# Sixteen rounds of a recommendation kernel: a hardware loop written out, with ids loaded ahead

## The chip, the cores and the metric

The kernel runs on one core of one Trainium2 chip. The metric is the device time of one execution in microseconds: 16,796.05 us is the median of three runs before the change (16,795.29 to 16,816.24). A separate execution was recorded by the hardware profiler; the trace and all rows below are from it.

## The reference, cut to what matters

There are 16,384 samples with 69 user ids and one label id each, and a table `emb` of 100,001 rows of 96 floats.

```python
u = emb[batch_user]                       # [B, 69, 96]
ql = emb[batch_label[:, 0]]               # [B, 96]
q = broadcast(ql[:, None, :])
z = concatenate([q, u, q - u, q * u], -1) # [B, 69, 384]
h = dice(z @ W1 + b1, a1)                 # 64 wide; dice(x) = (a*(1-p) + p)*x, p = sigmoid(x)
att = (h @ W2 + b2) @ W3 + b3             # one weight per (sample, field)
pre = where(batch_user < 100000, u * att, 0)
pooled = einsum('gf,bfe->bge', window, pre)   # 69 fields into 10 groups
x = concatenate([pooled, ql], -1)         # [B, 1056]
y = dice(bn(x @ Wf1 + bf1)) -> dice(bn(. @ Wf2 + bf2)) -> . @ Wf3 + bf3
```

## The kernel before, in words

Tokens are the (sample, field) pairs in order. A block is 128 samples, which is 8,832 tokens or 69 tiles of 128 tokens. Eight blocks make a round, and sixteen rounds make the batch; the rounds are a hardware loop (`tc.For_i`, L406), so the program holds the instructions of one round, and every engine branches back at its end.

At the head of a round SyncE loads `ids` (L408), the 552 columns of user ids and 8 columns of label ids that the round needs, into a pool with one buffer, and VectorE makes `mask` from it (L410), which is 1 where an id counts. `res` (one row of 1,024 outputs) is stored by SyncE at the round's end (L429).

Every embedding row is brought by GpSimd, with one indirect DMA for 128 rows, all of them from one line (`gather`, L226): one for the block's labels (`q`) in `block_head`, and one for each tile of tokens (`u`) in `pair_part1`, 70 in a block and 560 in a round. The tiles are handled in nine pairs of chunks (a chunk is up to four tiles). `upool` has ten buffers of one pair each, so gathers may run some nine pairs ahead of their use.

`block_head` transposes `q` (L238), and makes the label's part of the first layer for each chunk (L246, L247). `pair_part1` transposes the gathered tiles on TensorE (L293), copies them to SBUF on ScalarE (L294), multiplies them by the label's row on VectorE (L262, L271), forms the hidden layer in `ph` (L298, L299) and applies Dice (L308 to L310). `pair_part2` forms the attention weights `patt` (L321, L323), scales the pooling windows `rw` (L331, L339) and adds the pooled sums into `acc` (L358), which VectorE copies out (L366). `top_net` (L377 to L403) is run once for each block, as a chain of small steps on TensorE, VectorE and ScalarE.

The pairs are software-pipelined: part 2 of a pair is written after part 1 of the next (`pend`, `finish`). Inside a round this goes on over block ends. At the end of a round `finish(pend)` is called with nothing beside it, then the result is stored, and the loop's branch follows. The order on each engine is made by a scheduler from the code; dependences between engines are semaphores. A gather also waits on one of eight semaphores that the gather eight places before it has used.

Of the kernel before, what the change touches and what calls it, by code (L numbers as in the profile page):

```python
"""DIN-style recommendation model (target attention over 69 fields, windowed pooling, Dice MLP).

Tokens are the (sample, field) pairs in row-major order. A block is 128 samples = 8832 tokens
= 69 tiles of 128 tokens; every offset inside a block depends on shapes alone.

Per tile of 128 tokens, one indirect DMA brings the embedding rows (tokens on partitions), and
TensorE transposes them. With Wq, Wu, Wd, Wp the four row blocks of W1,
    z @ W1 + b1 = u @ (Wu - Wd) + (q * u) @ Wp + (q @ (Wq + Wd) + b1),
where the last term is one row per sample. It rides in the first product: the rows of the samples
of a chunk (at most 9) lie below Wu - Wd in the stationary operand, and constant sample indicators  # L10
lie below u in the moving one.
    att = dice @ (W2 @ W3) + (b2 @ W3 + b3)
comes out with tokens on partitions, as the pooling needs it: for a tile,
    pooled[e, (sample, g)] += sum_token u[token, e] * att[token] * window[g, field(token)],
with window spread over the (at most 3) samples that the tile touches.
"""
# [18 lines left out]
P = 128  # L35
# [16 lines left out]
#: Chunks of tiles, two to a pair: the halves of the 128 partitions that H1 = 64 leaves.  # L52
# [3 lines left out]
#: Groups of samples whose pooled sums share a PSUM bank.  # L56
# [11 lines left out]
def sample_rows():  # L68
    """[NS, tokens]: 1 where a token belongs to the chunk's n-th sample."""
    rows = np.zeros((NS, BLK * F), np.float32)  # L70
    for ch, s0 in zip(CHUNKS, S0):
        at = np.arange(ch[0] * P, (ch[-1] + 1) * P)
        rows[at // F - s0, at] = 1.0
    return rows


def tile_samples():
    """[P, NT, 3]: 1 where a tile's p-th token belongs to the tile's n-th sample."""
    at = np.arange(BLK * F)
    n = at // F - (at // P * P) // F  # L80
    return np.eye(3, dtype=np.float32)[n].reshape(NT, P, 3).transpose(1, 0, 2).copy()
# [3 lines left out]
def rec_kernel(  # L85
# [31 lines left out]
    # The attention net's weights.  # L117
# [36 lines left out]
    # W2 @ W3, once for each half of the partitions, and b2 @ W3 + b3.  # L154
# [14 lines left out]
    # The pooling windows of the samples of each tile.  # L169
    R = const.tile([P, NT, 3 * G], F32, name="R")  # L170

    # The top net's weights.
# [43 lines left out]
    ipool = ctx.enter_context(tc.tile_pool(name="ipool", bufs=1))  # L216
# [16 lines left out]
    def block_head(bi, ids):  # L233
        """The block's labels: qT, and the rows q @ (Wq + Wd) + b1 of each chunk's samples."""
        q = bpool.tile([P, E], F32, tag="q", name=f"q{bi}")
        gather(q, ids[:, NB * NT + bi : NB * NT + bi + 1])
        pq = ps_m.tile([E, BLK], F32, tag="m", name=f"pq{bi}")
        nc.tensor.transpose(pq, q, ident)  # L238
        qT = bpool.tile([E, BLK], F32, tag="qT", name=f"qT{bi}")
        nc.vector.tensor_copy(qT, pq)  # L240
        per = 6
        for k0 in range(0, NCH, per):
            pc = ps_m.tile([P, per, H1], F32, tag="m", name=f"pc{bi}_{k0}")
            for k in range(per):
                s0 = S0[k0 + k]
                nc.tensor.matmul(pc[E : E + NS, k, :], qT[:, s0 : s0 + NS], Cq, start=True, stop=True)  # L246
            nc.vector.tensor_tensor(  # L247
                caug[bi % 2][E : E + NS, k0 : k0 + per, :],
                pc[E : E + NS],
                b1r[E : E + NS].to_broadcast([NS, per, H1]),  # L250
                ALU.add,
            )
        return qT

    def times_q(dst, src, t0, n, qT):
        """dst = src * q over a chunk's tokens, t0 the first token in the block."""
# [22 lines left out]
    def pair_part1(bi, pr, ids, qT):  # L279
        """Gather, transpose, and the attention net's hidden layer: its Dice outputs."""  # L280
# [32 lines left out]
    def pair_part2(bi, pr, mask, u, y, acc):  # L313
        """Attention weights, and the pooled sums of the pair's tiles."""
# [91 lines left out]
    with tc.For_i(0, NIT, 1) as it:  # L406
        ids = ipool.tile([P, NB * (NT + 1)], I32, name="ids")
        nc.sync.dma_start(out=ids, in_=idx[bass.ds(it, 1)].rearrange("o p n -> (o p) n"))  # L408
        mask = ipool.tile([P, NB * NT], F32, name="mask")
        nc.vector.tensor_scalar(mask, ids[:, 0 : NB * NT], float(ITEM_NUM), None, ALU.is_lt)  # L410
        res = ipool.tile([1, NB * BLK], F32, name="res")

        def finish(pend):
            bi, pr, u, y, acc, qT = pend
            pair_part2(bi, pr, mask, u, y, acc)
            if pr == NCH // 2 - 1:
                top_net(bi, acc["pooled"], qT, res)

        pend = None
        for bi in range(NB):  # L420
            qT = block_head(bi, ids)
            acc = {"pooled": bpool.tile([E, G, BLK], F32, tag="pooled", name=f"pooled{bi}")}
            for pr in range(NCH // 2):
# [3 lines left out]
                pend = (bi, pr, u, y, acc, qT)  # L427
        finish(pend)
        nc.sync.dma_start(out=out_v[bass.ds(it, 1)], in_=res)  # L429
# [42 lines left out]
```

## Time and profile before

| | |
|---|---|
| runs, median of 3 | 16,796.05 us |
| lowest, highest | 16,795.29, 16,816.24 us |
| profiled execution, first to last instruction (span) | 12,197.5 us |
| the profiled execution's own time beside its span | not given by the page |
| median less the span | 4,598.55 us |
| TensorE, matmuls busy | 11,517.2 us, 94% |
| GpSimd busy | 8,693.8 us, 71% |
| VectorE busy, ScalarE busy | 3,956.7 us and 3,145.7 us |
| mean granted TensorE clock | 0.693 of full speed |

The span counts from the first to the last instruction that the profiler saw. The medians are of executions that were not profiled. Busy time of an engine is the time in which one of its instructions runs; time between two instructions is told by the view of waits, with what seems to have ended it.

### The profile page before, as it was taken

Reading aid. Unit: us, or ns where it says so; the run is one execution under the profiler, and the core shown is the slowest. Engines: PE = TensorE matmul, PEld = TensorE weight load, DVE = VectorE, ACT = ScalarE, POOL = GpSimd, SP = SyncE. Lnnn points to the kernel's source line nnn. Section 1 sums busy time; section 2 is a strip of 40 time slices with the busy share of each in tenths; the row PEclk is TensorE's granted clock in tenths of the full one; section 3 lists DMA queues with packets and bytes.
Section 4 is the critical chain, followed back from the end, with each engine's and each line's share of the span. In section 5 each row is a group of like instructions: output and inputs, shape, how many; then the busy total and the mean of one; then the engine's idle time right before and its main releaser. Section 6 shows DMA issues by size and latency. Waiting matters only on the chain. (4 is left out here: it accounts for less than half of the span.)

```text
span 12197.5 us, 145905 instructions
## 1 busy us (share of the span) xinstructions
PE 11517.2 (94%) x56708; PEld 7206.8 (59%) x56708; DVE 3956.7 (32%) x12194; ACT 3145.7 (26%) x5536; POOL 8693.8 (71%) x8966
## 2 busy tenths in 40 slices
PE   8999999999999999999999999999999999999999
PEld 5655656566565665656656566565565655656556
DVE  2333323333232333333323333333333333333333
ACT  2222222222222222222222222222222222222222
POOL 6767677676776767767677676776767767677676
PEclk7677767666676776666766676676766767666677
DMA  1111111111111111111111111111111111111111
GB/s 43 40 35 39 36 38 39 35 39 35 38 39 34 39 35 39 39 33 39 35 39 39 34 39 35 39 40 35 39 35 39 40 35 39 33 40 39 34 39 34
DMA packets 293219, 456.88 MB, mean 37 GB/s; under 512 B 145632, under 2 KB 146834, under 8 KB 292530
## 3 DMA queue, kind: packets, MB, share of 16 engines
q0 software_dynamic: 286720, 440.98, 17.3%
q8 instruction: 464, 7.60, 0.3%
q1 hardware_dynamic: 4144, 5.09, 0.2%
q14 instruction: 225, 1.84, 0.1%
q10 hardware_dynamic: 1666, 1.37, 0.0%
HBM read 446.79 MB, written 0.07 MB: 37 GB/s over the span
## 5 line engine op out<-in xcount | busy, mean ns | idle before, releaser
L226 POOL DMA_INDIRECT u<-in_emb,ids x8832 | 8569.7, 970 | 2691.6 <-issue 2459.1
L298 PE MATMUL ph<-uT,caug 105*64 105x512 f32 (+2 forms) x4608 | 3101.9, 808 | 2.6 <-ACT uT L294 2.0
L299 PE MATMUL ph<-quT,w 96*64 96x512 f32 (+2 forms) x4608 | 3019.7, 796 | 0.4 <-DVE quT L271 0.4
L358 PEld LDWEIGHTS acc<-rw,u 128*96 128x96 f32 x18176 | 2515.6, 237 | 608.1 <-issue 234.7
L293 PEld LDWEIGHTS ptr<-ident,u 128*96 128x96 f32 x8832 | 1225.2, 164 | 2467.1 <-issue 1781.1
L358 PE MATMUL acc<-rw,u 128*96 128x30 f32 (+2 forms) x18176 | 2565.7, 305 | 33.2 <-DVE rw L339 32.3
L293 PE MATMUL ptr<-ident,u 128*96 128x128 f32 x8832 | 2095.6, 352 | 347.5 <-DMA u<-in_emb,ids 337.0
L294 ACT COPY uT<-ptr 96x512 f32<-96x512 f32 (+2 forms) x2304 | 1280.8, 560 | 3778.6 <-PE ptr L293 3775.9
L308 ACT ACTIVATE g<-ph 128x512 f32<-128x512 f32 (+2 forms) x1280 | 720.2, 563 | 4438.8 <-PE ph L299 4137.0
L321 PEld LDWEIGHTS patt<-v,y 128*128 128x128 f32 x8704 | 1451.4, 250 | 352.0 <-issue 291.1
L321 PE MATMUL patt<-v,y 128*128 128x2 f32 x8704 | 1445.1, 287 | 3.9 <-DVE y L310 1.8
L331 DVE SCALAR_TENSOR_TENSOR w<-patt,bb,mask 128x8 f32<-128x8 f32 (+2 forms) x1280 | 274.8, 223 | 3571.9 <-PE patt L321 3363.1
L262 DVE TENSOR_TENSOR quT<-uT,qT 96x414 f32<-96x414 f32 (+3 forms) x2304 | 1363.7, 592 | 7.9 <-ACT uT L294 6.9
L310 DVE TENSOR_TENSOR y<-ph,g 128x512 f32<-128x512 f32 (+2 forms) x1280 | 823.0, 643 | 799.8 <-ACT g L309 794.4
L271 DVE TENSOR_TENSOR quT<-uT,qT 96x29 f32<-96x29 f32 (+33 forms) x4352 | 751.0, 185 | 869.3 <-ACT uT L294 742.7
L299 PEld LDWEIGHTS ph<-quT,w 96*64 96x64 f32 x4608 | 621.2, 171 | 695.2 <-issue 498.6
L309 ACT ACTIVATE g<-g,a1c,na1c 128x512 f32<-128x512 f32 (+2 forms) x1280 | 999.4, 781 | 20.7
L377 PE MATMUL p<-pooled,wf 96*100 96x128 f32 x5120 | 736.6, 309 | 19.5 <-DVE pooled L366 15.2
L377 PEld LDWEIGHTS p<-pooled,wf 96*100 96x100 f32 x5120 | 709.6, 199 | 28.0 <-DVE pooled L366 17.0
L366 DVE COPY pooled<-acc 96x430 f32<-96x430 f32 (+1 forms) x384 | 340.6, 887 | 1126.8 <-PE acc L358 1126.8
L298 PEld LDWEIGHTS ph<-uT,caug 105*64 105x64 f32 x4608 | 532.8, 168 | 279.6 <-issue 165.3
L226 POOL DMA_INDIRECT q<-in_emb,ids x128 | 123.5, 965 | 769.1 <-DVE mask L410 735.0
(53 smaller groups left out, 2926.9 us busy)
## 6 DMA issues: line engine op xcount, KB each, us to landing
u<-in_emb,ids POOLq DMA_INDIRECT x8832, 2.5
ids<-in_idx SPq DMA_DIRECT2D x16, 280.0 KB
q<-in_emb,ids POOLq DMA_INDIRECT x128, 2.5
wf<-in_Wf ACTq DMA_DIRECT2D x1, 825.0 KB
wt<-in_wtok ACTq DMA_DIRECT2D x1, 345.0 KB
uT<-in_rows SPq DMA_DIRECT2D x16, 18.0 KB
out<-res SPq DMA_DIRECT2D x16, 4.0 KB
ts<-in_tsamp ACTq DMA_DIRECT2D x1, 103.5 KB
```

The source lines that it names most:

```text
L226: nc.gpsimd.indirect_dma_start(out=dst, out_offset=None, in_=emb, in_offset=bass.IndirectOffsetOnAxis(ap=index, axis=0),)
L262: nc.vector.tensor_tensor(dst[:, at : at + m * F].rearrange("e (m f) -> e m f", f=F), src[:, at : at + m * F].rearrange("e (m f) -> e m f" ...
L271: nc.vector.tensor_tensor(dst[:, at : at + m], src[:, at : at + m], qT[:, s : s + 1].to_broadcast([E, m]), ALU.mult,)
L293: nc.tensor.transpose(ptr[:, i * P : (i + 1) * P], u[:, 4 * j + i, :], ident)
L294: nc.scalar.copy(uT[k][0:E, :], ptr[:, 0:n])
L298: nc.tensor.matmul(o, caug[bi % 2][:, k, :], uT[k], start=True, stop=False)
L299: nc.tensor.matmul(o, Wp, quT[:, 0:n], start=False, stop=True)
L309: nc.scalar.activation(gs, gs, AF.Identity, bias=a1c[lo:hi], scale=na1c[lo:hi])
L310: nc.vector.tensor_mul(y[lo:hi, 0:n], ph[lo:hi, 0:n], gs)
L321: nc.tensor.matmul(patt[:, :, i], y[:, cols], v2, start=True, stop=True)
L358: nc.tensor.matmul(acc[gi][:, (x - a) * G : (z - a) * G], u[:, 4 * j + i, :], rw[:, j, i, (x - lo) * G : (z - lo) * G], start=False, stop= ...
L377: nc.tensor.matmul(p1[:, i, :], wf1[:, k, i * DH : (i + 1) * DH], pooled[:, k, :] if k < G else qT, start=(k == 0), stop=(k == G),)
```

## The change

The 16 rounds are written out in Python (`for it in range(NIT)`), so the program holds all 16 and has no branch. `pend` now carries the mask, the result row and the round's number, and is no longer finished at a round's end: part 2 of a round's last pair stands after part 1 of the next round's first pair, as it did at block ends. The pool of `ids`, `mask` and `res` has two buffers. The next round's ids are loaded in the code after the fifth block of a round; the store of `res` is issued when its round's last pair is finished. In the first round alone, seven of the eight label gathers are issued as two gathers of fewer rows each (64 and 64, 126 and 2, 124 and 4, and so on), for which the ids have eight more columns. Comments and the text at the file's head were taken out, with lines kept empty, so that L226 of the kernel before is L229 of the changed one.

On GpSimd, before: the end of the loop's body. The names are buffers, with the block and the pair in front (`u7_8` is block 7, pair 8).

```order
L226 DMA u7_6_4655<-in_emb,ids_221 128x96 x8
L226 DMA u7_7_4715<-in_emb,ids_221 128x96 x8
L226 DMA u7_8_4771<-in_emb,ids_221 128x96 x5
L406 REGISTER_ALU
L406 COMPARE_AND_BRANCH
L406 UNCONDITIONAL_BRANCH
```

On GpSimd, changed: the last label's gathers of the first round and the first pair behind them; further on, the end of the first round.

```order
L229 DMA q7_4237<-in_emb,ids0_209 125x96
L229 DMA q7_4237<-in_emb,ids0_209 3x96
L229 DMA u7_0_4269<-in_emb,ids0_209 128x96 x8
...
L229 DMA u7_7_4712<-in_emb,ids0_209 128x96 x8
L229 DMA u7_8_4768<-in_emb,ids0_209 128x96 x5
L229 DMA q0_4823<-in_emb,ids1_3069 128x96
L229 DMA u0_0_4854<-in_emb,ids1_3069 128x96 x8
L229 DMA u0_1_4952<-in_emb,ids1_3069 128x96 x8
```

The branch and the register step between `u7_8` and `q0` are gone, and one gather stands in front of the next; the label of the first round's last block comes by a gather of 125 rows and one of 3.

On SyncE the loop's body was one ids load and one store. Now two ids loads stand at the start, and each later load stands ahead of the store of the round before it (the load of the third round's `ids2`, then the store of the first round's `res0`).

On TensorE, before: the last instructions of the loop's body, from the pooled sums of block 7's last pair on.

```order
L358 MATMUL acc7_2_4711<-rw7_8_4828,u7_8_4771 96x30 x4
L358 MATMUL acc7_2_4711<-rw7_8_4828,u7_8_4771 96x20
L377 MATMUL p1_7_4841<-pooled7_4271,wf1_131 100x128 x10
L377 MATMUL p1_7_4841<-qT7_4245,wf1_131 100x128
...
L395 MATMUL p2_7_4872<-x1_7_4839,wf2_133 80x128 x2
L402 MATMUL p3_7_4879<-x2_7_4870,wf3_135 1x128
L406 REGISTER_ALU
L406 COMPARE_AND_BRANCH
L406 UNCONDITIONAL_BRANCH
```

On TensorE, changed: around the end of the first round. `ptr0_2`, `ptr0_3`, `ph0_0` and `ph0_1` are of the second round, `acc7_2` and `p1_7` belong to the first.

```order
L304 MATMUL ph0_0_4855<-uT1_77,caug0_67 64x512
L305 MATMUL ph0_0_4855<-quT0_0_1_4881,w1_63 64x512
L299 MATMUL ptr0_2_1_5028<-ident_58,u0_2_5010 96x128
L364 MATMUL acc7_2_4708<-rw7_8_4897,u7_8_4768 96x30 x4
L364 MATMUL acc7_2_4708<-rw7_8_4897,u7_8_4768 96x20
L299 MATMUL ptr0_2_1_5028<-ident_58,u0_2_5010 96x128 x2
L299 MATMUL ptr0_3_0_5068<-ident_58,u0_3_5066 96x128 x4
L383 MATMUL p1_7_4910<-pooled0_7_4268,wf1_131 100x128 x10
L383 MATMUL p1_7_4910<-qT7_4242,wf1_131 100x128
...
L305 MATMUL ph0_1_4953<-quT0_1_0_4964,w1_63 64x512
```

Transposes and products of the next round's pairs now stand ahead of and between the pooled sums and the top net of the last block.

```diff
@@ -49,11 +49,14 @@
 S_DICE = float(1.0 / np.sqrt(1.0 + 1e-9))
 S_BN = float(1.0 / np.sqrt(1.0 + 1e-5))
 
 CHUNKS = [list(range(4 * k, 4 * k + 4)) for k in range(16)] + [[64, 65, 66], [67, 68]]
 NCH = len(CHUNKS)
 S0 = [min(c[0] * P // F, BLK - NS) for c in CHUNKS]
+
+LABEL_ROWS = [128, 64, 126, 124, 120, 112, 96, 125]
+NCOL = NB * (NT + 2)
+
 GROUPS = [(0, 43), (43, 86), (86, 128)]
 
 
...
@@ -213,7 +216,7 @@
         nc.tensor.matmul(pb, b2m, w3, start=True, stop=True)
         nc.vector.tensor_add(bb, pb, b3r)
 
-    ipool = ctx.enter_context(tc.tile_pool(name="ipool", bufs=1))
+    ipool = ctx.enter_context(tc.tile_pool(name="ipool", bufs=2))
     upool = ctx.enter_context(tc.tile_pool(name="upool", bufs=10))
     bpool = ctx.enter_context(tc.tile_pool(name="bpool", bufs=2))
     cpool = ctx.enter_context(tc.tile_pool(name="cpool", bufs=3))
...
@@ -230,10 +233,13 @@
             in_offset=bass.IndirectOffsetOnAxis(ap=index, axis=0),
         )
 
-    def block_head(bi, ids):
-        """The block's labels: qT, and the rows q @ (Wq + Wd) + b1 of each chunk's samples."""
+    def block_head(it, bi, ids):
+
         q = bpool.tile([P, E], F32, tag="q", name=f"q{bi}")
-        gather(q, ids[:, NB * NT + bi : NB * NT + bi + 1])
+        first = LABEL_ROWS[bi] if it == 0 else P
+        gather(q[0:first], ids[0:first, NB * NT + bi : NB * NT + bi + 1])
+        if first < P:
+            gather(q[first:P], ids[0 : P - first, NB * (NT + 1) + bi : NB * (NT + 1) + bi + 1])
         pq = ps_m.tile([E, BLK], F32, tag="m", name=f"pq{bi}")
         nc.tensor.transpose(pq, q, ident)
         qT = bpool.tile([E, BLK], F32, tag="qT", name=f"qT{bi}")
...
@@ -403,30 +409,39 @@
         nc.vector.tensor_scalar(res[:, bi * BLK : (bi + 1) * BLK], p3, bf3c, None, ALU.add)
 
     out_v = out.rearrange("(n b) o -> n (o b)", n=NIT)
-    with tc.For_i(0, NIT, 1) as it:
-        ids = ipool.tile([P, NB * (NT + 1)], I32, name="ids")
-        nc.sync.dma_start(out=ids, in_=idx[bass.ds(it, 1)].rearrange("o p n -> (o p) n"))
-        mask = ipool.tile([P, NB * NT], F32, name="mask")
+
+    def finish(pend):
+        bi, pr, u, y, acc, qT, mask, res, it = pend
+        pair_part2(bi, pr, mask, u, y, acc)
+        if pr == NCH // 2 - 1:
+            top_net(bi, acc["pooled"], qT, res)
+            if bi == NB - 1:
+                nc.sync.dma_start(out=out_v[it : it + 1], in_=res)
+
+    def load_ids(it):
+        ids = ipool.tile([P, NCOL], I32, tag="ids", name=f"ids{it}")
+        nc.sync.dma_start(out=ids, in_=idx[it : it + 1].rearrange("o p n -> (o p) n"))
+        return ids
+
+    pend = None
+    ids = load_ids(0)
+    for it in range(NIT):
+        mask = ipool.tile([P, NB * NT], F32, tag="mask", name=f"mask{it}")
         nc.vector.tensor_scalar(mask, ids[:, 0 : NB * NT], float(ITEM_NUM), None, ALU.is_lt)
-        res = ipool.tile([1, NB * BLK], F32, name="res")
-
-        def finish(pend):
-            bi, pr, u, y, acc, qT = pend
-            pair_part2(bi, pr, mask, u, y, acc)
-            if pr == NCH // 2 - 1:
-                top_net(bi, acc["pooled"], qT, res)
-
-        pend = None
+        res = ipool.tile([1, NB * BLK], F32, tag="res", name=f"res{it}")
         for bi in range(NB):
-            qT = block_head(bi, ids)
-            acc = {"pooled": bpool.tile([E, G, BLK], F32, tag="pooled", name=f"pooled{bi}")}
+            qT = block_head(it, bi, ids)
+            acc = {"pooled": bpool.tile([E, G, BLK], F32, tag="pooled", name=f"pooled{it}_{bi}")}
             for pr in range(NCH // 2):
                 u, y = pair_part1(bi, pr, ids, qT)
                 if pend is not None:
                     finish(pend)
-                pend = (bi, pr, u, y, acc, qT)
-        finish(pend)
-        nc.sync.dma_start(out=out_v[bass.ds(it, 1)], in_=res)
+                pend = (bi, pr, u, y, acc, qT, mask, res, it)
+            if bi == NB // 2 and it + 1 < NIT:
+                ids_next = load_ids(it + 1)
+        if it + 1 < NIT:
+            ids = ids_next
+    finish(pend)
 
 
 def kernel(**inputs):
...
@@ -436,8 +451,9 @@
     x = {k.removeprefix("L0_rec_").removeprefix("r_"): np.asarray(v) for k, v in inputs.items()}
     tokens = x["batch_user"].reshape(NIT, NB, NT, P).transpose(0, 3, 1, 2).reshape(NIT, P, NB * NT)
     labels = x["batch_label"].reshape(NIT, NB, BLK).transpose(0, 2, 1)
+    rest = np.stack([np.roll(labels[:, :, b], -LABEL_ROWS[b], axis=1) for b in range(NB)], axis=2)
     arrays = {
-        "idx": np.concatenate([tokens, labels], axis=2),
+        "idx": np.concatenate([tokens, labels, rest], axis=2),
         "emb": x["emb"],
         "W1": x["W1"],
         "b1": x["b1"],
```

## Rows read from the trace of the kernel before

**Rows 1.** The page: span; busy time, share and instructions of each engine; clock

```profile
span 12197.5 us, 145905 instructions
PE 11517.2 (94%) x56708; PEld 7206.8 (59%) x56708; DVE 3956.7 (32%) x12194; ACT 3145.7 (26%) x5536; POOL 8693.8 (71%) x8966
...
core 0: 12197.5 us, clock 0.693
```

**Rows 2.** Waits: engine and line, what ended it: us, times, longest

```profile
POOL u L226 <- issue: 2459.1, 8069, 0.3
...
POOL q L226 <- DVE mask L410: 735.0, 16, 58.0
...
PE ptr L293 <- DMA u<-in_emb,ids: 337.0, 426, 1.6
...
POOL u L226 <- DMA u<-in_emb,ids: 143.8, 472, 0.3
...
PE pq L238 <- DMA q<-in_emb,ids: 87.6, 16, 7.1
...
POOL u L226 <- PE ptr L293: 36.9, 121, 0.3
```

**Rows 3.** Windows, first gather to last, of each round (16): first, last, sum

```profile
core 0: us, PE busy (x) PEld busy (x) DVE busy (x) ACT busy (x) POOL busy (x), PEclk, DMA share, GB/s
25.54:738.10 712.56, 691.68 (x3371) 427.54 (x3372) 235.04 (x724) 185.73 (x327) 542.20 (x560) 0.70 0.19 39
...
11441.52:12155.12 713.60, 680.25 (x3367) 422.29 (x3367) 234.28 (x723) 185.36 (x327) 543.24 (x560) 0.70 0.19 39
sum 11418.82, PE 10971.22 PEld 6799.21 DVE 3743.73 ACT 2963.96 POOL 8693.08; mean PE 685.70 PEld 424.95 DVE 233.98 ACT 185.25 POOL 543.32
```

**Rows 4.** Windows, last gather to the next (15 round ends): first, longest, sum

```profile
738.10:780.73 42.63, 29.37 (x175) 22.85 (x173) 11.96 (x37) 10.62 (x19) 0.00 (x0) 0.74 0.04 9
...
10617.97:10675.99 58.02, 45.23 (x211) 31.44 (x211) 14.74 (x46) 12.61 (x22) 0.00 (x1) 0.62 0.03 7
...
sum 710.76, PE 514.79 PEld 383.53 DVE 194.34 ACT 170.70 POOL 0.03; mean PE 34.32 PEld 25.57 DVE 12.96 ACT 11.38 POOL 0.00
```

**Rows 5.** Timeline around the second round end: start, us, instruction [idle before, releaser]

```profile
1493.30 0.94 POOL L226 DMA_INDIRECT u<-in_emb,ids  x1 [0.30 <-issue]
...
1510.28 2.71 PE L358 MATMUL acc<-rw,u 128*96 128x30 f32 x16 [1.23 <-DVE rw L339]
...
1531.77 0.34 DVE L403 TENSOR_SCALAR res<-p,bf3c 1x128 f32<-1x128 f32 x1 [0.68 <-PE p L402]
1532.14 0.26 SPq L429 DMA_DIRECT2D out<-res  x1
...
1534.98 0.36 SPq L408 DMA_DIRECT2D ids<-in_idx  x1
1537.91 0.45 DVE L410 TENSOR_SCALAR mask<-ids 128x552 f32<-128x552 int32 x1 [5.80 <-DMA ids<-in_idx]
1538.63 0.94 POOL L226 DMA_INDIRECT q<-in_emb,ids  x1 [44.39 <-DVE mask L410]
1539.88 0.94 POOL L226 DMA_INDIRECT u<-in_emb,ids  x1 [0.30 <-issue]
```

**Rows 6.** The gathers of one line: duration ns min/median/max; time to landing

```profile
L226 POOL DMA_INDIRECT u<-in_emb,ids x8832: 940/944/2267, 26.9 to 12154.2; - x197
...
DMA to landing us min/median/max: 2.3/2.5/4.2
```

**Rows 7.** DMA queues (packets, MB, share of 16 engines); issues of the ids

```profile
q8 instruction: 464, 7.60, 0.3%
...
q14 instruction: 225, 1.84, 0.1%
...
ids<-in_idx SPq DMA_DIRECT2D x16, 280.0 KB
```

## The prediction

> **What bounds the kernel now.** I read the page first, and it misleads: TensorE's matmuls are busy 94% of the span, GpSimd 71% [rows 1], so TensorE seems to be the bound. The view of waits corrects this. GpSimd's 8,832 gathers of tiles have 2,459 us of idle time before them that nothing ends but the issue of the next one, 0.3 us each [rows 2]; with 8,693.8 us of busy time [rows 1] and 735 us of waits for the mask [rows 2], GpSimd is either gathering, issuing, or standing at a round's end. TensorE in turn waits for gathers (337 us before transposes), while the gathers' waits that are put down to TensorE's transposes come to 36.9 us, none above the 0.3 us that any issue takes [rows 2]: the buffers of `upool` are never full. TensorE follows the gathers.
>
> The windows give the same as a sum. From a round's first gather to its last pass 712.56 to 713.60 us in the two rounds shown, 11,418.8 us over all sixteen [rows 3]: 713.7 us a round, 1.274 us a gather (560 a round). Between a round's last gather and the next round's first lie 42.6 to 58.0 us in which GpSimd does nothing, 710.8 us for fifteen ends [rows 4], 47.4 us each. The first gather begins at 25.5 us, and from the last one's end to the span's end are 12,197.5 - 12,155.1 = 42.4 us [rows 1, 3]. The sum 25.5 + 11,418.8 + 710.8 + 42.4 = 12,197.5 is the span, so each term that the change touches can be priced by itself.
>
> The timeline shows what a round's end consists of [rows 5]: the last gather starts at 1493.30; its tile goes through the pair's chain; pooled sums are still added at 1510.28; the top net ends with `res` at 1531.77; the store is issued, then the ids load at 1534.98; the mask follows at 1537.91, and the first gather at 1538.63. It is one chain with no other block's work beside it.
>
> Here the reading of busy time decides the sum. If TensorE were the bound, only its own idle time at round ends would go, 710.8 - 514.8 = 196 us [rows 4]; by the gathers it is all of the 710.8. The Trainium skill (Trainium Kernel Development and Optimization, Performance Expectations) holds that matmul busy time is a bad measure of distance to the limit because matmuls are pipelined. The trace agrees: 94% busy goes with waits for gathers.
>
> **Own time and the runs.** The profiled span is 12,197.5 us, the median of the runs 16,796.05; the difference of 4,598.5 us is in no row. I take it as a constant that lies around the work, since the three runs agree within 21 us; its other readings are rivals below. The Trainium skill (Runtime: NRT & Kernel Launch, The ~15µs preamble/postamble breakdown) gives some 9 to 15 us for start and end of a launch. By that the runs should lie near 12,210, and no run here does; the measurement decides, and the sum goes by the difference above.
>
> **The change, part by part.**
>
> Round ends. The branch and the wait for the mask between `u7_8` and `q0` go on GpSimd, and the ids are there half a round earlier. What is late next at a round's end is only the next gather's issue, 0.3 us [rows 2]. Removed: 710.8 us. Added: 15 x 0.3 = 4.5 us. Nothing of the chain of the last pair and the top net is taken away; it now runs beside the next round's gathers, as at the 112 block ends inside rounds, which are part of the 713.7 us.
>
> Cover for that. TensorE has 514.8 us of work in the fifteen windows [rows 4] that must now fit beside gathers. If TensorE could not catch up, `upool` would fill and gathers would wait for it. In rounds it is busy 10,971 of 11,419 us at a granted clock of about 0.70 [rows 3], between its two levels 1.2 and 2.4 GHz; it waits there, so it keeps pace at the clock it gets. Its mean clock must rise by some 5% (11,517 us of work in 11,500). From below it costs nothing, if the clock rises as it falls behind; from above, it gains no more from a higher clock than the 448 us that it idles in rounds now, and up to 514.8 - 448 = 67 us stay as waits of gathers. I take nothing, because its waits for gathers are spread over rounds, and keep +67 for the range.
>
> The 7 more gathers of the first round. Price 1.274 us each [rows 3], 8.9 us. With fewer rows they may be cheaper (none below 0, as they are added), or slower: the longest time to landing is 4.2 us [rows 6], 7 x 4.2 = 29 us. I take 8.9, the nearest row. Behind a label's gathers wait `pq` on TensorE and the tiles' gathers on GpSimd.
>
> ids, masks, stores. The load moves on SyncE ahead of the store of the round before, so a store waits until the last gathers of that round have read the buffer; nobody waits for a store but the second next round's `res`. The mask on VectorE waits for the load, with quT products and `x1` queued behind it; the row before is 735 us for sixteen masks, but all of that came after the round's end [rows 2, 5]. Now the load is issued when the round's last gather is done and takes the 2.9 us from 1534.98 to 1537.91 [rows 5]; the mask stands some twenty gathers later in VectorE's order, 25 us. Bounds: 0 to 15 x 2.9 = 44 us; I take 0, since that wait would have to reach GpSimd through a full `upool`. The ids grow from 280 KB [rows 7] by 4 KB a round, on a queue that is idle.
>
> Instructions. One round's program becomes sixteen; but the loop has read its instructions anew as well: 7.60 + 1.84 MB fetched [rows 7] are 65 bytes for each of the 145,905 instructions that ran [rows 1], so each was fetched about once for each time it ran. The changed kernel runs about as many. Price 0.
>
> VectorE's nearness. Gathers take 944 ns as a median and up to 2,267 [rows 6]. Their mean of 1.274 us already holds what they suffer beside the other engines. VectorE's 194 us of round-end work [rows 4] come beside gathers now; at the rate of rounds, (1.274 - 0.944 - 0.30) x 8,960 = 269 us for 3,743.7 us of VectorE work [rows 3], this is 14 us. From below 0. I take 14.
>
> Sum: -710.8 + 4.5 + 8.9 + 14 = -683 us; span 11,514 us; with 4,598.5 around it 16,113 us, which I round to 16,110. Cost bounds: with +67, +20 (slow label gathers) and +44, 16,244; without the 14 and the 8.9, 16,090.
>
> **The rivals.**
>
> A. The runs are the profiled execution stretched, all of it, by 16,796 / 12,197.5 = 1.377. For: the three runs agree as one steady pace would. Against: nothing in the rows is slower than another time it runs. Then 683 x 1.377 = 940 us go: 15,856.
>
> B. The runs have TensorE at 1.2 GHz throughout. The profile's mean clock is 0.693; at 0.5 the span would be 12,197.5 x 0.693 / 0.5 = 16,906, close to the median. Against: the clock rose in every round of the trace [rows 3], and the busy share would be no lower in the runs. TensorE is then the bound, and the change frees its idle time at round ends, 196 us [rows 4], and its waits for the first label of a round, 88 us [rows 2]: 16,512.
>
> C, the other side. What lies around the work grows with the program. If the 4,598.5 us were spent on moving inputs and program at one rate, the table (100,001 x 96 x 4 bytes = 38.4 MB), ids (16 x 280 KB = 4.6 MB), about 1.5 MB of weights and constants and 0.6 MB of program (one sixteenth of 9.4) make 45 MB, 102 us for one MB. Sixteen rounds of program add 8.8 MB, 900 us: 17,010, slower. It decides from 683 / 8.8 = 78 us for one MB on. Against: no row shows a program moved before the work; its instructions are fetched during the span [rows 7].
>
> D. VectorE locks gathers out. The longest gather is 1.32 us above the median [rows 6]. If each of the some 38 VectorE instructions of a round end [rows 4] cost a gather that much, 15 x 38 x 1.32 = 752 us come back, 16,850. The Trainium skill (SBUF — State Buffer, SBUF: two separate sides) says that a GpSimd-issued DMA beside a VectorE copy can take five times as long. The trace agrees that some gathers are longer, but its mean is only 35% above the median with the issue in it, so I give this little.
>
> E. It does not do what it says: the gathers of a new round stop for the old round's `upool` buffers, and the gap stays. Then 16,796 + 9. Against: after a gap the waits for TensorE in rounds are 0.3 us [rows 2].
>
> F. The loop costs the runs more than the trace shows (4,598.5 / 16 = 287 us a round); up to that goes too, below 15,800.
>
> **How the numbers follow.** Forecast 0.56, A 0.13, B 0.13, C 0.06, D 0.02, E 0.04, F 0.06. A measurement tells 0.2%, 34 us, from no change. Faster are the forecast, A, B and F: 0.88. Same is E, 0.04; slower C and D, 0.08. The forecast's own range is 16,080 to 16,250. For eight in ten A and B come in, so 15,820 to 16,530; F, C, D and E lie outside.
>
> **What would show it.** Gathers back to back over round ends, 1.25 to 1.28 us from start to start; no wait of `q` for the mask; a span of about 11,514; idle GpSimd only at both ends. TensorE's mean clock should be above 0.693, about 0.73. If the span falls by some 680 and the median by as much, the difference is a constant; by 940, it is A; by under 300, B. Waits of gathers for TensorE longer than 0.3 us would prove the cover wrong, and a span down with a median up would be C.

## Result and the profile after

| | before | after |
|---|---|---|
| runs, median | 16,804.82 us (4 runs) | 16,118.06 us (4 runs, 16,082.94 to 16,191.10) |
| ratio, 95% interval | | 0.9597 [0.9573, 0.9621] |
| profiled execution: its run, its span | | 16,191.10, 16,189.3 us |

The change takes 687 us off, and the forecast was 16,110 us. One sentence must stand ahead of all that follows: the same program needs some 12,200 us on one chip and 16,800 to 17,000 us on others (that it is the chip itself, and not what it was in at the time, is not shown); by their times the trace of before [rows 1 to 7] is of the first kind, the runs in the table and the trace of after are of the second. I call them the 12,200 chip and the 16,800 chips. The two traces can therefore not be subtracted from each other; the experiments supply the missing partners on each side.

First the page and the clock of after, against [rows 1]: span, busy time, the chain's shares, mean granted clock.

```profile
span 16189.3 us, 144750 instructions
PE 12511.9 (77%) x56708; PEld 8013.8 (50%) x56708; DVE 3926.3 (24%) x12194; ACT 3123.8 (19%) x5506; POOL 8572.5 (53%) x8973
PE 60%; another core or an unknown queue 29%; issue 4%; DVE 3%; ACT 3%; POOL 1%; DMA 0%; SPq 0%; DVEq 0%; ACTq 0%; POOLq 0%
core 0: 16189.3 us, clock 0.598
```

The span is the whole run but for 1.8 us. VectorE, ScalarE and GpSimd have the same busy time as in [rows 1] within 1.4%; TensorE has 995 us more at a clock of 0.598 in place of 0.693, and 29% of the chain is put down to something unknown. Next the waits of after (us, times, longest), against [rows 2]:

```profile
POOL u L229 <- PE ptr L299: 2421.4, 366, 23.1
POOL u L229 <- issue: 2292.2, 7414, 20.9
POOL u L229 <- PE acc L364: 2043.7, 354, 24.8
...
POOL q L229 <- DVE mask L430: 23.0, 1, 23.0
```

The gathers wait for TensorE, 4,465 us for `ptr` and `acc` together, up to 24.8 us at a time; in [rows 2] it was 36.9 us for `ptr`, and never over 0.3. Here TensorE paces and the gathers follow. The sixteen waits for the mask have become one, the first round's. The windows, cut as in [rows 3] (first, second and last round, sum) and [rows 4] (second end, sum):

```profile
24.36:970.90 946.54, 721.96 (x3111) 437.29 (x3113) 216.68 (x667) 172.71 (x304) 543.25 (x567) 0.60 0.14 30
971.21:1965.64 994.43, 765.42 (x3540) 490.07 (x3536) 244.25 (x758) 194.89 (x344) 535.25 (x560) 0.61 0.14 29
...
15071.79:16080.92 1009.13, 758.44 (x3541) 489.46 (x3537) 244.60 (x760) 194.56 (x344) 533.73 (x560) 0.61 0.13 28
sum 16051.99, PE 12406.86 PEld 7941.62 DVE 3887.25 ACT 3097.45 POOL 8571.74; mean PE 775.43 PEld 496.35 DVE 242.95 ACT 193.59 POOL 535.73
```

```profile
1965.64:1965.95 0.31, 0.31 (x3) 0.29 (x2) 0.00 (x0) 0.19 (x1) 0.01 (x1) 0.50 0.00 0
...
sum 4.57, PE 4.57 PEld 4.02 DVE 1.90 ACT 2.02 POOL 0.04; mean PE 0.30 PEld 0.27 DVE 0.13 ACT 0.13 POOL 0.00
```

The fifteen ends are 4.57 us together, the 15 x 0.3 us of issue that the prediction put there, against 710.76 [rows 4]. But a round takes 1,003 us in place of 713.7. The timeline at the second end, against [rows 5]:

```profile
1964.70 0.95 POOL L229 DMA_INDIRECT u<-in_emb,ids  x1 [0.30 <-issue]
1965.95 0.95 POOL L229 DMA_INDIRECT u<-in_emb,ids  x1 [0.30 <-issue]
...
1968.63 0.33 SPq L423 DMA_DIRECT2D ids<-in_idx  x1
1971.99 0.94 POOL L229 DMA_INDIRECT u<-in_emb,ids  x1 [5.09 <-PE ptr L299]
```

1.25 us from start to start across the end. The very next gather then waits 5.1 us for TensorE, because the pool is full. The windows are cut by count (560 gathers a round), and from the second end on they are one gather early: a label's gather, which before stood right in front of its block's first tile, now has 61 other gathers between it and that tile, so the gather at 1965.95 is the second round's last tile. The two remaining groups, the gathers' durations [rows 6] and the queues [rows 7]:

```profile
L229 POOL DMA_INDIRECT u<-in_emb,ids x8832: 939/947/1439, 25.9 to 16080.0; - x197
```

```profile
q8 instruction: 453, 7.42, 0.2%
q14 instruction: 225, 1.84, 0.0%
...
ids<-in_idx SPq DMA_DIRECT2D x16, 284.0 KB
```

A gather costs what it did, and the sixteenfold program fetches no more instructions than the loop. What differs is TensorE. One stretch of after shows how (start, duration, instruction, idle before and releaser):

```profile
5055.12 1.97 PE L305 MATMUL ph<-quT,w 96*64 96x512 f32 x2
...
5058.76 1.87 PE L327 MATMUL patt<-v,y 128*128 128x2 f32 x8
...
5079.15 0.60 ACT L314 ACTIVATE g<-ph 128x512 f32<-128x512 f32 x1 [25.30 <-remote]
...
5082.58 1.97 PE L304 MATMUL ph<-uT,caug 105*64 105x512 f32 x2 [21.96 <-ACT uT L300]
...
5084.23 0.23 DVE L337 SCALAR_TENSOR_TENSOR w<-patt,bb,mask 128x8 f32<-128x8 f32 x1 [29.65 <-remote]
```

By its record the product of L305 is done at 5057.09; ScalarE, which waits for it, starts 22.1 us later. The `patt` of 5060.63 is taken up by VectorE at 5084.23. "Remote" is the view's name for a release that no record explains; since no engine but GpSimd has a record between 5060.63 and 5079.15, I read it as TensorE signalling later than the modelled end of its matmul. There are 202 such waits at L314, 3,264 us. The Trainium skill (TensorE: Matmul & The Clock Gate, Seeing it yourself) warns that clock records have been observed to be unreliable on this chip. No run here shows which record is wrong.

### The profile page after: what moved, and what is told of

It reads as the page before. It is cut to its first block, busy times and chain, and to the rows that moved or that the text cites. A ratio compares the mean times of both kernels' runs of the same rounds, so it can differ in the third digit from the quotient of the medians.

```text
span 16189.3 us, 144750 instructions
## 1 busy us (share of the span) xinstructions
PE 12511.9 (77%) x56708; PEld 8013.8 (50%) x56708; DVE 3926.3 (24%) x12194; ACT 3123.8 (19%) x5506; POOL 8572.5 (53%) x8973
## 4 chain that ended last, share of the span: by engine, by line
PE 60%; another core or an unknown queue 29%; issue 4%; DVE 3%; ACT 3%; POOL 1%; DMA 0%; SPq 0%; DVEq 0%; ACTq 0%; POOLq 0%
PE acc L364 14%; PE ph L305 11%; PE ph L304 10%; PE ptr L299 10%; PE patt L327 7%; PE pc L252 3%; PE p L383 3%; ACT g L315 1%; DVE y L316 1%; ACT g L314 1%; DVE pooled L372 1%; PE p L401 1%; ACT uT L300 1%; POOL u L229 1%
## 5 line engine op out<-in xcount | busy, mean ns | idle before, releaser
L229 POOL DMA_INDIRECT u<-in_emb,ids x8832 | 8442.8, 956 | 7443.9 <-PE ptr L299 2421.4
L304 PE MATMUL ph<-uT,caug 105*64 105x512 f32 (+2 forms) x4608 | 3332.6, 894 | 2298.3 <-ACT uT L300 1640.5
L305 PE MATMUL ph<-quT,w 96*64 96x512 f32 (+2 forms) x4608 | 3264.4, 866 | 213.7 <-DVE quT L277 185.3
L364 PEld LDWEIGHTS acc<-rw,u 128*96 128x96 f32 x18176 | 2810.6, 261 | 1142.5 <-issue 522.8
L364 PE MATMUL acc<-rw,u 128*96 128x30 f32 (+2 forms) x18176 | 2853.9, 325 | 391.7 <-DVE rw L345 317.8
L299 PEld LDWEIGHTS ptr<-ident,u 128*96 128x96 f32 x8832 | 1411.3, 185 | 2518.3 <-issue 2070.5
L299 PE MATMUL ptr<-ident,u 128*96 128x128 f32 x8832 | 2290.2, 395 | 178.4 <-issue 106.9
L314 ACT ACTIVATE g<-ph 128x512 f32<-128x512 f32 (+2 forms) x1280 | 719.4, 562 | 6345.9 <-remote 3263.5
L304 PEld LDWEIGHTS ph<-uT,caug 105*64 105x64 f32 x4608 | 573.2, 183 | 2632.9 <-ACT uT L300 1707.8
L327 PEld LDWEIGHTS patt<-v,y 128*128 128x128 f32 x8704 | 1660.0, 284 | 266.4 <-issue 154.5
L327 PE MATMUL patt<-v,y 128*128 128x2 f32 x8704 | 1620.8, 309 | 124.1 <-DVE y L316 116.3
L305 PEld LDWEIGHTS ph<-quT,w 96*64 96x64 f32 x4608 | 641.6, 183 | 822.5 <-issue 444.7
L252 PE MATMUL pc<-Cq,qT 96*9 96x64 f32 x4608 | 520.3, 305 | 378.0 <-DVE qT L246 201.5
```

The costliest lines, as they stand in the source:

```text
L229: nc.gpsimd.indirect_dma_start(out=dst, out_offset=None, in_=emb, in_offset=bass.IndirectOffsetOnAxis(ap=index, axis=0),)
L299: nc.tensor.transpose(ptr[:, i * P : (i + 1) * P], u[:, 4 * j + i, :], ident)
L304: nc.tensor.matmul(o, caug[bi % 2][:, k, :], uT[k], start=True, stop=False)
L305: nc.tensor.matmul(o, Wp, quT[:, 0:n], start=False, stop=True)
L327: nc.tensor.matmul(patt[:, :, i], y[:, cols], v2, start=True, stop=True)
L364: nc.tensor.matmul(acc[gi][:, (x - a) * G : (z - a) * G], u[:, 4 * j + i, :], rw[:, j, i, (x - lo) * G : (z - lo) * G], start=False, stop= ...
```

## Experiments

Theory G: GpSimd's gathers pace the work, and what lies around it is constant. Theory T: in the timed runs TensorE is slower and paces.

**1. The kernel before, once more (12,200 chip).** No edit.

> The kernel before, unchanged, with a profile of its own. Theory G (the prediction's: gathers pace the work, 4,598 us lie around it): span 12,190 to 12,210, first gather to last of a round 714 us, gathers never wait for TensorE, time 16,800. Theory T (in the runs TensorE is slower than in the first trace and paces the work, nothing lies around it): span 16,790 to 16,820, within 5 us of the time, some 1,000 us from first gather to last of a round, gathers waiting for TensorE by 1,500 us or more.

Measured: 12,261.24 us, span 12,259.5, beside 12,212.31 (median of 9, 12,191.24 to 12,240.95). The trace of before is no oddity, and nothing like 4,598 us lies around a span: 1.7 us. Neither theory foresaw the time: G had the span nearly right (50 us low) and 4,500 us too much around it, T had nothing around it and the span 4,500 us too long.

**2. Without the split label gathers (12,200 chip).**

```diff
-        first = LABEL_ROWS[bi] if it == 0 else P
+        first = P
```

> The changed kernel with every label gathered by one gather (seven gathers fewer, in the first round). Theory G: 9 us faster than the changed kernel, 16,109 (0.9587 of before). Theory T: GpSimd has slack, so no difference from the changed kernel, 16,118 within its spread of 50.

Measured: 11,503.73 us, ratio 0.9418 [0.9405, 0.9431]. The sums of its windows, rounds and then ends, and its waits:

```profile
sum 11384.86, PE 11079.38 PEld 7179.05 DVE 3908.66 ACT 3089.10 POOL 8659.13; mean PE 692.46 PEld 448.69 DVE 244.29 ACT 193.07 POOL 541.20
...
sum 4.55, PE 4.55 PEld 3.25 DVE 1.21 ACT 0.66 POOL 0.03; mean PE 0.30 PEld 0.22 DVE 0.08 ACT 0.04 POOL 0.00
```

```profile
POOL u L229 <- issue: 2434.6, 7989, 0.3
...
POOL u L229 <- PE ptr L299: 30.5, 100, 0.3
POOL q L229 <- DVE mask L430: 23.2, 1, 23.2
```

This is the prediction's sum made real: 24.5 + 11,384.9 + 4.55 + 50.0 = 11,463.9 of span, with no wait of a gather for TensorE above 0.3 us. On this chip G holds, though TensorE is close behind: its matmuls are busy for 11,126.2 us, 97% of the span. The expected 9 us cannot be read, since the changed kernel was not run on this chip.

**3. Half of the ends (12,200 chip).** A loop of eight, two rounds in its body, the pair carried and the ids ahead between these two only.

```diff
-    with tc.For_i(0, NIT, 1) as it:
+    with tc.For_i(0, NIT // 2, 1) as it:
+        for r in range(2):
...
+                if bi == NB // 2 and r == 0:
+                    ids_next = load_ids(1)
```

> A hardware loop of 8 with two rounds in its body: ids double-buffered and pairs carried over inside the body, so 8 of the 15 inner round ends lose their gap and 7 keep it; no split labels. Theory G: 8/15 of 697 us, 372 us below before, 16,430. Theory T with the cost in the round ends alone: 8/15 of the 687 us measured, 366 us, 16,438: the same. If the cost lay in the hardware loop's program (its fetching, its branch) at any length, less: 8/16 of it at most.

Measured: 11,922.94 us, ratio 0.9764 [0.9747, 0.9781], 289 us off. An end that remains, and the sum of fifteen:

```profile
1453.08:1511.57 58.49, 45.62 (x212) 31.72 (x212) 14.77 (x46) 12.62 (x22) 0.00 (x0) 0.62 0.04 12
...
sum 389.50, PE 298.11 PEld 211.36 DVE 100.59 ACT 87.61 POOL 0.03; mean PE 19.87 PEld 14.09 DVE 6.71 ACT 5.84 POOL 0.00
```

Less than the expected 372 because the seven that remain take (389.5 - 8 x 0.3) / 7 = 55.3 us each, not 47.4: a saving of 321 in these rows. One end is not one fixed price; it holds what TensorE has still to do. By size alone, 289 of the 709 us of experiment 2, it would suit a cost of the loop's program too (at most half); that the eight ends inside the body are down to 0.3 us speaks for the ends.

**4. Unrolled, ids ahead, the pair drained at each end (12,200 chip).** No split either.

```diff
-    finish(pend)
+        finish(pend)
+        pend = None
```

> The changed kernel (no split labels), unrolled and ids ahead, but the last pair of each round is finished before the next round's first pair is written. Theory G: gathers do not stop for it, since their order has no gap: within 100 us of the changed kernel, 16,118 to 16,220. Theory T: TensorE loses time where the last pair's chain and the top net stand alone; between 0 (the scheduler mixes them with the next round's gathered tiles) and the 687 us of the whole change; I expect 200, 16,320.

Measured: 11,764.58 us, ratio 0.9639 [0.9609, 0.9669]. Theory G, within 100 us of the changed kernel, missed: it is 261 us over experiment 2, nearer to T's 200. The gathers cross the end without a gap but are stopped later:

```profile
POOL u L229 <- PE acc L364: 295.0, 79, 18.1
```

So 448 us come from unrolling with ids ahead, 261 more from the carried pair (17 an end): where the pair is drained, what TensorE loses there comes back as waits for a free `u`.

**5. The changed kernel as it is (a 16,800 chip).** No edit.

> The changed kernel as it is, beside the kernel before on one chip; its only difference to the kernel without split label gathers (11,503.7 us, at 12,212 us before) is 7 more gathers of the first round. Theory G, gathers pace the work: where the kernel before takes some 12,200 us, 7 x 1.274 = 8.9 us more, 11,513, with gathers back to back over round ends. Rival: a small gather costs as much as a long landing, 4.2 us, 11,533. Theory T, TensorE paces the work: where the kernel before takes some 16,800 us, 16,118, with the gathers waiting for TensorE some 4,400 us in all; the split then costs nothing.

Measured: 16,366.50 us, ratio 0.9644 [0.9616, 0.9672], beside 16,974.80. Theory T's side of the expectation, 250 us high; the gathers wait for `ptr` and `acc` by 2,681.7 + 1,664.1 = 4,346 us, near the 4,400.

**6. Ids late, and 7. ids late and drained (same chip).** Neither has the split, and the early load is taken out; experiment 7 also drains the pair, as in experiment 4.

```diff
+    idpool = ctx.enter_context(tc.tile_pool(name="idpool", bufs=1))
...
     for it in range(NIT):
+        ids = load_ids(it)
```

> Unrolled, no split of label gathers, the last pair carried over the round's end, but the ids are loaded at the round's head into one buffer, so the load waits for the last gather of the round before. Theory G: each of 15 ends has a gap of landing (2.3 us), load (2.9 us) and mask and issue (0.7 us) = 5.9 us, 11,504 + 89 = 11,593 where the kernel before takes some 12,200. Rival V: the mask stands in VectorE's order behind the last block's pooled sums, some 17 us after the last gather, so the gap is 17 to 25 us and the time 11,760 to 11,880. Theory T, TensorE paces: full buffers hide the gap, under 20 us more than without it.

> Unrolled, no split of label gathers, last pair drained at the round's end and ids loaded at its head: the kernel before without its loop instruction alone. Theory G with rival V: the gap is the chain from the last gather to the mask, 38 to 47 us an end, 12,080 to 12,210 where the kernel before takes some 12,200. Rival L, the loop itself (its branch and the engines' meeting there) makes most of the gap, and the data's order little: the drained kernel's 11,765 plus 89 for the load, 11,854.

Measured: 16,159.52 us, ratio 0.9525 [0.9492, 0.9558], and 16,165.52 us, 0.9533 [0.9501, 0.9565]. Each is the unrolled kernel with one or both of the other two parts undone, and both are some 200 us faster than the changed kernel. The second end and the sum of the ends of experiment 7, and what its gathers wait for there:

```profile
1995.42:2000.69 5.27, 5.27 (x20) 2.43 (x19) 1.28 (x6) 1.27 (x2) 0.01 (x2) 0.50 0.25 65
...
sum 79.63, PE 77.64 PEld 42.50 DVE 25.19 ACT 21.92 POOL 0.04; mean PE 5.18 PEld 2.83 DVE 1.68 ACT 1.46 POOL 0.00
...
POOL q L230 <- DMA ids<-in_idx: 102.0, 16, 22.4
```

The times of the expectations were for a 12,200 chip; what still tells the theories apart is the gap. It is 5.3 us, near the 5.9 of landing, load, mask and issue, and not the 17 to 47 us of rival V. V fell because a gather waits for the ids to land and not for the mask: the second round's gathers start at 984.98, its mask at 1036.4. That leaves rival L: without the loop instruction the long gap is gone. What in the loop makes it is not separated. In the trace of before ScalarE and TensorE, too, are let into the next round only there, by the loop's line, at the time of the ids load (1534.98 in [rows 5]):

```profile
1534.82 1.28 ACT L294 ACT_TABLE_LOAD   x1 [4.04 <-PEq L406]
...
1534.86 0.94 PE L354 MATMUL acc<-zrow 1*96 1x430 bf16 x2 [3.13 <-PEq L406]
```

So the engines meet at the loop's end. But in the unrolled program SyncE also issues the load ahead of the store of the round before (981.33 and 1120.75 in experiment 7), where in the loop it stands behind it. On this chip the unrolling alone gives all of the gain; on a 12,200 chip it was not run alone. The Trainium skill (Runtime: NRT & Kernel Launch, Instruction fetch mechanics) gives as a reason for full unrolling that a taken branch forces a fetch of its target, where that lies outside the two pages at hand. By that rule the gap would lie at the branch, behind the store; between the store and the load are only 2.8 us, 1532.14 to 1534.98 [rows 5], and most of the window lies ahead of the store and is the last pairs' work.

**8. Half of the gathers (same chip).**

```diff
-                gather(u[:, 4 * j + i, :], ids[:, bi * NT + t : bi * NT + t + 1])
+                if i % 2 == 0:
+                    gather(u[:, 4 * j + i, :], ids[:, bi * NT + t : bi * NT + t + 1])
```

> Left out: every second tile's gather; its transposes and products read the neighbouring tile's rows, so TensorE, VectorE and ScalarE do the same instructions with half of the 8,832 row gathers. Theory G: GpSimd's pace goes and TensorE's is what is left; at the clock seen so far (0.69) its 11,126 us of matmul time stay, 11,150, and if its clock rises because it no longer waits for gathers, 11,126 x 0.69 = 7,700 us at the least. Theory T, TensorE already paces: no shorter than with all gathers, 11,480 to 11,510.

The transposes and the products of those tiles read the neighbour's rows, and the split is left out. Measured: 10,748.42 us, one run. This fells theory T as I had it: TensorE, with the same instructions on a 16,800 chip, is no slower than on the other. The next three were made to see whether that stands and why.

**9. The kernel before, for its trace on a 16,800 chip, 10. without the split, 11. half of the gathers.** Edits as above (11 as 8); all on one other chip.

> The kernel before once more, to have its trace where its runs take some 16,800 us (if this chip is such a one; else 12,200 us and the rows already known). Theory T, TensorE's late completions pace that condition: GpSimd waits for TensorE within rounds for some 3,000 us or more (37 us in the first trace), the windows of round ends still hold about 45 us each without a gather (15 x 45 = 680 us), and TensorE is idle for over 500 us in them. Rival: the rounds are as short as in the first trace, 713.7 us, and 4,500 us lie around the work.

> The changed kernel without the split label gathers again. Where the kernel before takes 12,200 us: 11,504, ratio 0.942. Where it takes 16,800 to 17,000: theory split, the 7 extra gathers or what they displace cost the 206 us between 16,366 with split and 16,160 with late ids and without split, so a ratio of 0.952; theory late, the late load is what is faster there, so the ratio of the changed kernel, 0.964, stays.

> Left out again: every second tile's gather, TensorE's work unchanged. It took 10,748 us once, beside a kernel before at 16,975. Theory T as I had it (TensorE's completions are slow by the condition of the chip, whatever GpSimd does): that one run fell into a quick spell, and where the kernel before takes some 16,900 this one takes 15,000 to 16,200, a ratio over 0.88. Theory S (TensorE is slowed only together with the gathers, so halving them gives its pace back): 10,700 to 10,800 in each round, ratio 0.63 to 0.64. Where the kernel before takes 12,200, both give 10,700 and a ratio of 0.88.

Measured: 16,838.43 us (beside 16,826.09, median of 7); 16,082.43 us, ratio 0.9556 [0.9510, 0.9603]; 10,975.89 us, ratio 0.6524 [0.6498, 0.6551]. First a wait of the kernel before, against the 735.0 of [rows 2]; then its windows (a round, the sum; an end, the sum), and the sum of the rounds without split, with TensorE's wait for `uT` there:

```profile
POOL q L226 <- DVE mask L410: 1493.9, 16, 107.3
```

```profile
1072.75:2013.74 940.99, 714.34 (x3123) 431.28 (x3124) 217.91 (x669) 171.46 (x303) 536.72 (x560) 0.60 0.15 30
...
sum 15246.39, PE 11579.37 PEld 6977.73 DVE 3474.34 ACT 2752.89 POOL 8577.81; mean PE 723.71 PEld 436.11 DVE 217.15 ACT 172.06 POOL 536.11
...
2013.74:2109.63 95.89, 80.77 (x423) 56.69 (x421) 29.81 (x92) 24.34 (x44) 0.00 (x0) 0.71 0.02 4
...
sum 1469.78, PE 1261.47 PEld 879.32 DVE 456.90 ACT 363.54 POOL 0.04; mean PE 84.10 PEld 58.62 DVE 30.46 ACT 24.24 POOL 0.00
```

```profile
sum 15985.45, PE 12377.89 PEld 7914.60 DVE 3888.01 ACT 3098.51 POOL 8571.86; mean PE 773.62 PEld 494.66 DVE 243.00 ACT 193.66 POOL 535.74
...
PE ph L304 <- ACT uT L300: 1353.7, 99, 25.2
```

On this chip an end takes 98.0 us, twice that of [rows 4], because TensorE has 84 us of work left when the last gather is done, where it had 34 [rows 4]. The expectation of theory T had ends of 45 us with over 500 us of idle TensorE in them; it is idle for 1,469.8 - 1,261.5 = 208 us there. The rival, rounds of 713.7 us, is out. The change takes 1,470 - 4.6 = 1,465 us of ends away, and the rounds grow by 15,985 - 15,246 = 739: that work goes into the rounds, since TensorE paces there. Net 726, and the spans differ by 731. This is most likely where the 687 us of the result come from, too; on the result's chip there is no trace of before. The 726 can be split by TensorE's records: its idle time falls by 268 us, and its busy time, rounds and ends together, from 12,841 to 12,382, by 458 us for as many instructions. What makes them shorter is not shown. The granted clock is 0.71 in that end without gathers and 0.60 in the round beside it.

The split's part is not settled by the ratio: 0.9556 lies between the expected 0.952 and 0.964, and its interval holds only the first, but the changed kernel, with the split, had 0.9597 in the result and 0.9644 in experiment 5. Experiments 5 and 6, on one chip, say more: from the first gather of a round to that of the next, the first round, which has the 7 extra gathers, takes 967 and 970 us, while the 14 after it take 1,017 and 1,003 on average. So the 207 us between them lie where there is no split, and what makes them (the early ids, and with them the place of the label gathers, are the other difference) is open. Experiment 11 gives 0.6524, a little over theory S's 0.64 and far under T's 0.88: halving the gathers gives TensorE its pace back.

**12. Half of the gathers by plain loads (16,800 chip).** All tiles and bytes are brought in, half of them by SyncE, from rows in table order.

```diff
+                else:
+                    r0 = (bi * NT + t) * P
+                    nc.sync.dma_start(out=u[:, 4 * j + i, :], in_=emb[r0 : r0 + P, :])
```

> Changed: without the split label gathers, every second tile's rows come by a plain load of 128 consecutive table rows, issued on SyncE, in place of a gather (so other rows than the ids name); as many tiles, bytes and buffers as with all gathers, half of GpSimd's gathers, TensorE's work the same. Leaving those tiles out altogether gave 10,976 beside a kernel before at 16,826. Theory D, the bytes brought in slow TensorE's completions: where the kernel before takes some 16,800 us, 15,500 to 16,200 as with all gathers. Theory S, GpSimd's gathers do (their number, or that TensorE waits upon them): 10,900 to 11,200. Where the kernel before takes some 12,200 us both give 10,700 to 11,100, TensorE's pace, 400 us or more under the 11,504 with all gathers, if the gathers were what paced them.

Measured: 11,071.37 us, ratio 0.6507 [0.6478, 0.6536]. Its bytes, its clock and TensorE's first wait:

```profile
DMA packets 780672, 457.08 MB, mean 41 GB/s; under 512 B 702688, under 2 KB 703890, under 8 KB 779954
...
core 0: 11089.2 us, clock 0.713
...
PE ph L308 <- ACT uT L304: 93.7, 47, 3.4
```

The bytes are not it: at 41 GB/s, more than the 28 of after, TensorE keeps a clock of 0.713, and its wait for `uT`, 1,353.7 us in experiment 10, is 93.7. (They come in 2.7 times as many packets.) What takes TensorE's pace away on the 16,800 chips goes with the number of GpSimd's gathers. Whether it is their instructions, or the rhythm in which tiles then come, stays open, as does what sets these chips apart; halving the gathers on a 12,200 chip was not run.

## Why the prediction was right, and where it was not

**The step that failed** is the first number of the sum: "I take it as a constant that lies around the work". Around the span lie 1.7 to 2.1 us in each run whose time and trace are on record. In the trace of experiment 9 rounds take 952.9 us in place of 713.7 and ends 98.0 in place of 47.4: 16 x 239.2 + 15 x 50.6 = 4,586 us, which is nearly all of the 4,639 us between the two spans. It lay in the work, on chips where TensorE's completions come late. The Trainium skill's 9 to 15 us for start and end (Runtime: NRT & Kernel Launch, The ~15µs preamble/postamble breakdown) was the better guide: by it the runs had to lie near the span, and the difference asked for another execution, not for a constant. The measured 1.7 to 2.1 us are less than that page's figure, and decide.

**Bound.** "TensorE follows the gathers" is right for the profiled chip (experiment 2) and wrong for the timed ones, where gathers wait 4,465 us for TensorE. Of the rivals B comes nearest: TensorE as the bound at a granted clock of 0.60, not 0.5. Its price, 196 + 88 = 284 us of TensorE's idle time, is near the 268 us by which that falls from experiment 9 to 10; what it missed are the 458 us by which TensorE's busy time falls, which it held constant.

**Round ends.** -710.8 + 4.5 is confirmed on the 12,200 chip: 4.55 us remain, and 709 are measured against 692 without the label gathers, -710.8 + 4.5 + 14. On the timed chips it is -1,465 in ends and +739 in rounds. That 683 forecast and 687 measured agree there is luck: two differences that cancel, and no support for the step.

**Cover.** It held where gathers pace (30.5 us of waits for `ptr`, none above 0.3; nothing of the +67), but not in the way forecast: the clock stayed at 0.690 instead of 0.73. TensorE's matmul time fell instead, from 11,517 to 11,126 us for as many instructions: of the 4,608 products of one line (L298 before, L304 after) 2,632 began at the higher of its two levels, where it had been 2,487. Whether that explains the fall is not shown: from experiment 9 to 10 the busy time falls as well, with 1,551 and 1,559 such products. On the 16,800 chips the cover was wrong by the prediction's own sign: waits up to 24.8 us.

**The small terms.** VectorE's nearness (+14) did not come: rounds fell by 34 us, 11,418.8 to 11,384.9, and GpSimd's busy time in them by as much, 8,693.1 to 8,659.1. The label gathers (8.9) were not run on a 12,200 chip, and on the others the round that has them is not longer. No gather waits for the mask beyond the first. The larger program fetches no more, as said.

## What to carry to other kernels

Where a profile's span and the median of the runs differ by more than a few us, the profile is likely of another condition, as here: get a trace of an execution that the median speaks of before any row is priced. What a gap is worth is read from the engine that paces. If the engine that stands idle in it paces, the gap is worth all of itself; if another engine paces and works through the gap, that work comes back in the rounds, and only the rest is gained. Who paces is read from waits, not from busy shares: 94% busy, TensorE still followed. Halving the supplier then showed what the waits could not, that the pace of TensorE itself goes with the number of gathers.

## What the runs showed of the hardware

- One program took 12,212 us on one chip and 16,826 to 16,993 us (medians) on two others, the runs of a set within 1% of each other, with busy times on GpSimd, VectorE and ScalarE equal within 1.7%.
- On the latter, engines that wait for TensorE started up to 20 us and more after the modelled ends of its records (5057.09 and 5079.15), and halving GpSimd's gathers brought the time to 10,976 us, under that of the quicker chip with all gathers.
- With half of the gathers by plain loads as many bytes took 11,071 us: the gathers, not the transfers, go with TensorE's loss.
- A loop's end left the gathers idle for 47.4 us on the one chip and 98.0 on one of the others, where TensorE had more work left; unrolled, with the load waiting for the round's last gather, it was 5.3 on the third.
